# A fixed issue order for TensorE, VectorE and ScalarE in the first stage of a Mamba, attention and mixture-of-experts layer

## The chip, the cores and the metric

The kernel runs on one core of a Trainium2 chip. That core has a matrix engine (TensorE, PE in the profile), a vector engine (VectorE, DVE), a scalar engine for activations (ScalarE, ACT), a general engine (GpSimd, POOL) and a synchronising engine (SyncE, SP) whose queue issues nearly all transfers here. Each engine takes its own list of instructions[...]. The metric is the time of one execution on the device in microseconds (us); less is better. The time before is the median of three executions, 5567.89 us (5564.01 to 5571.6).

## The reference, cut to what matters

Eight sequences of 512 tokens with 512 features pass through three blocks, each followed by a residual sum and a layer norm. Everything is in 32-bit floats.

```python
x = _layernorm(x + mamba(x))             # state-space block
x = _layernorm(x + attention(x, ctx))    # 16 heads of 32, keys and values from ctx
x = _layernorm(x + moe(x))               # 32 experts, 4 per token, capacity 640, plus a shared expert
```

The state-space block projects to 1024 inner channels and a gate, convolves over four taps, forms a step size `dt` (a softplus), and runs a recurrence over the tokens for 1024 channels times 16 states, then gates and projects back:

```python
dA = exp(A[None, None] * dt[..., None]);  dBx = dt[..., None] * B_ssm[:, :, None, :] * x_main[..., None]
h = dA_t * h + dBx_t                     # token by token
y_t = einsum('bdn,bn->bd', h, C_t)
y = (y + x_main * D) * silu(z);  out = y @ out_proj_w + residual
```

The expert block takes a softmax over 32 logits, keeps four of eight groups and four experts in them, numbers the tokens of each expert in order, and drops those beyond 640.

## The kernel before, in words

`program` (from L1423) opens three stages in turn: `layers` (state-space block, attention, gate, shared expert), `experts` (the 32 experts) and `finish` (the last layer norm). Only `layers` is touched by the change.

**The main loop of `layers`.** The tokens are cut into 16 chunks of 256, two per sequence. A chunk is walked in 32 steps; a step handles 128 channels (`c = 2*q + ci`) and four states (`g`). One step is: `carry` (ACT, L443: the incoming state into column 0 of a buffer `h`, of which there are four), `decays` (ACT, L437: four exponentials for the *next* step into one of two buffers `l_da`), `scan` (DVE, L449 product, L453 the recurrence, and in the first chunk of a sequence L455, a copy of the last state), then other work, and last `collect` (DVE, L470: `h` times C in place; PE, L474: four products that sum over the states into the PSUM tile `py`, of which there is one; in the first state group also two products at L462).

**The other work of a step** is of two kinds, and stands in the text between `scan` and `collect`. Some belongs to the same chain: for the chunk before, `back` (PE, L503, steps 1 and 2) with its residual sum and layer norm (DVE L512, then L74 to L78, ACT L57, L58, L80); for this chunk, `gate_x` (PE L302, steps 3 to 6); for the chunk after, `norm_x` (step 9), `flip_x` (step 11), `convolve` (steps 12, 15, 18, 21: PE L302, then ACT L322 and L328, then six taps on DVE, L336), `silu` (step 23), `x_proj` (step 24); and every eighth step `prepare` (PE L389, then seven ACT instructions, L399 to L405, then four on DVE, L409 to L412, whose results transfers spread over `both`). The rest are the *units* of the sequence before, made by `units` (L706): queries, score maxima (PE L766, DVE L768), their negation (PE L775, ACT L779), weights (PE L792, ACT L796), weighted sums (PE L808, ACT L820), division (ACT L837, L838, DVE L839 to L841), output (PE L703, DVE L856, L857), the gate (`choose`, DVE L546 to L602; `locate`, DVE L620 to L635) and the shared expert (PE L703, DVE L883, L897). A budget of weights, one number per unit, decides how many units fall into each step, so that they end with the second chunk. The units of the last sequence follow after the main loop, with no scan beside them.

**How a unit is written down.** `do` (L1006) issues a unit's matmuls and then runs what was left over of the units before, so that the reading of a PSUM tile stands one unit behind its matmuls; `settle` runs what is left and keeps what that returns in turn; `dry` repeats until nothing is left. `settle` also stands right ahead of `collect`:

```python
            h = carry(t, 2 * q + ci, g)
            ...
            scan(t, 2 * q + ci, g, f["ready", q][1], bc, das[n % 2], h)
            ...                      # back, gate_x, prepare, convolve, units: each through do()
            settle()
            collect(2 * q + ci, g, h, bc, py, f)
```

PSUM: two buffers `mm` for projections and most units, two buffers `sc` for scores and weights, one `po`, one `py`.

**What sets the order.** The text of the kernel is not the order of the queues. The framework collects all instructions with what they depend on, and its scheduler plays the program through with its own estimates of durations; an engine takes next, among the instructions that are ready in that estimate, the one that stands first in the text. What comes out is one fixed list per engine, which the chip then follows. `silu` (L350) and its return to the table of exponentials (L354) are tied by `keep_in_program_order` behind what was written before them on ACT; nothing ties later instructions behind them. Transfers of `layers` are issued by SP (and the scattered ones by POOL), in an order that the same scheduler sets.

## Time and profile before

| | |
|---|---|
| median of three executions | 5567.89 us (5564.01 to 5571.6) |
| profiled execution, its own time | 5569.36 us |
| its span, first to last instruction | 5567.7 us |
| first scan starts, last scan ends (DVE L453) | 72.2 us, 3691.1 us |
| last product of the main loop ends (PE L474) | 3694.5 us |
| `layers` ends, `experts` begins | about 3947 us |
| PE busy over the span | 4880.6 us (88%) |
| DVE busy over the span | 4349.5 us (78%) |
| ACT busy over the span | 2592.1 us (47%) |
| granted TensorE clock, mean | 0.937 |

In the profile a line such as `L470 DVE TENSOR_TENSOR h<-h,bc` names the line of the kernel, the engine, the operation, and what is written from what. The timeline gives, for each merged group, its start, its length from first start to last end, and, in square brackets, the idle time of the engine just before it and what ended that. A matmul in 32-bit floats stands in the records as two, so that the four products of `collect` are eight.

### The profile page before, as it was taken

How to read it: one execution, taken by the hardware profiler on the slowest of the kernel's cores; microseconds unless marked ns; L12 is line 12 of the kernel's file. 1: busy time of each engine (PE TensorE's matmuls, PEld its weight loads, DVE VectorE, ACT ScalarE, POOL GpSimd, SP SyncE). 2: the span in 40 equal slices, each digit the busy share in tenths (PEclk: the TensorE clock that was granted, in tenths of full speed). 3: DMA queues.
4: the chain of work that ended last, by engine and by line, in shares of the span. 5: the costliest groups of instructions: out<-in, count | busy, mean ns of one | idle time of the engine just before them, and what ended most of it. 6: DMA issues, size and time to landing. Idle time of an engine off the chain costs nothing. (4 is left out here: it accounts for less than half of the span.)

```text
span 5567.7 us, 60361 instructions
## 1 busy us (share of the span) xinstructions
PE 4880.6 (88%) x19752; PEld 2718.5 (49%) x19752; DVE 4349.5 (78%) x5738; ACT 2592.1 (47%) x5481; POOL 569.2 (10%) x424
## 2 busy tenths in 40 slices
PE   6668889888888988888898898879899999999994
PEld 4334344334434434443443443333577777777773
DVE  6998899989889999898989999864466565555554
ACT  4555555655566455555555656523222222222223
POOL 1000002001100200200020020010111111111111
PEclk8778999999999999999999999989999999999997
DMA  6787355444634634643463454441345454544444
GB/s 187 226 229 211 109 137 176 121 118 143 178 106 112 201 97 129 184 124 108 122 207 98 120 188 113 112 158 45 96 125 126 124 126 119 126 125 120 119 121 145
DMA packets 554282, 769.83 MB, mean 138 GB/s; under 512 B 135754, under 2 KB 268394, under 8 KB 551920
## 3 DMA queue, kind: packets, MB, share of 16 engines
q1 hardware_dynamic: 517952, 677.55, 41.6%
q0 software_dynamic: 33280, 76.90, 7.4%
q10 hardware_dynamic: 2736, 11.54, 0.5%
q8 instruction: 156, 2.56, 0.2%
q14 instruction: 158, 1.29, 0.1%
HBM read 508.68 MB, written 165.05 MB: 121 GB/s over the span
## 5 line engine op out<-in xcount | busy, mean ns | idle before, releaser
L437 ACT ACTIVATE l_da<-both,l_aneg 128x256 f32<-128x256 f32 x2048 | 888.4, 499 | 790.6 <-DVE h L453 745.9
L453 DVE TENSOR_TENSOR_SCAN h<-l_da,h 128x1028 f32<-128x1028 f32 x512 | 1170.0, 2292 | 50.7 <-ACT h L443 27.3
L474 PE MATMUL py<-h,l_twice 128*64 128x256 f32 x4096 | 627.5, 421 | 195.1 <-DVE h L470 194.9
L449 DVE TENSOR_TENSOR h<-both,bc 128x1024 f32<-128x1024 f32 x512 | 617.9, 1214 | 142.5 <-PE py L474 81.6
L470 DVE TENSOR_TENSOR h<-h,bc 128x1024 f32<-128x1024 f32 x512 | 622.6, 1219 | 6.3 <-DMA l_ka<-filld 0.3
L474 PEld LDWEIGHTS py<-h,l_twice 128*64 128x64 f32 x4096 | 292.5, 147 | 568.8 <-issue 237.7
L1220 PE MATMUL ps_h<-xT,w 128*128 128x320 f32 x1536 | 435.6, 433 | 0.0
L766 PE MATMUL ps_s<-l_ka,l_qa 64*128 64x512 f32 x1024 | 314.1, 692 | 137.4 <-DVE mx L768 137.2
L1300 POOL DMA_INDIRECT based<-y,xe x160 | 252.1, 1576 | 1313.5 <-ACT y L1323 571.3
L1241 DVE TENSOR_TENSOR hT<-ps_h,p 128x320 f32<-128x320 f32 x128 | 62.9, 492 | 379.0 <-PE ps_h L1220 379.0
L768 DVE TENSOR_REDUCE mx<-ps_s 128x2 f32<-128x1024 f32 x256 | 310.4, 1216 | 55.4 <-PE ps_s L766 54.7
L1220 PEld LDWEIGHTS ps_h<-xT,w 128*128 128x128 f32 x1536 | 292.2, 190 | 118.2 <-issue 0.4
L792 PE MATMUL ps_t<-l_qa,l_ka 64*128 64x512 f32 x1024 | 299.6, 648 | 20.9 <-ACT eT L796 17.5
L796 ACT ACTIVATE eT<-ps_t 128x1024 f32<-128x1024 f32 x256 | 259.1, 1013 | 110.1 <-PE ps_t L792 109.6
L808 PE MATMUL po<-eT,l_va 128*64 128x512 f32 x1024 | 281.4, 629 | 24.5 <-ACT raw L820 20.8
L641 POOL DMA_INDIRECT xbuf<-x2t,dest x128 | 218.8, 1709 | 814.6 <-DVE dest L635 776.2
L1220 PE MATMUL ps_h<-t,s 128*128 128x320 f32 x1024 | 286.1, 432 | 0.0
L302 PE MATMUL ps_z<-xnT,wm 128*128 128x256 f32 x1024 | 240.9, 389 | 17.4 <-DVE o L512 16.4
L302 PE MATMUL ps_x<-xnT,wm 128*128 128x256 f32 x1024 | 245.6, 394 | 11.1 <-DMA wm<-in_in_proj_w 10.1
L703 PE MATMUL ps_p<-x2T,wa 128*128 128x512 f32 x512 | 243.9, 625 | 11.8 <-DVE hT L883 10.3
L503 PE MATMUL po<-wm,zs 128*128 128x512 f32 x512 | 236.9, 613 | 9.8 <-DVE k L688 5.3
L1220 PEld LDWEIGHTS ps_h<-t,s 128*128 128x128 f32 x1024 | 194.6, 190 | 81.1
(234 smaller groups left out, 7422.5 us busy)
## 6 DMA issues: line engine op xcount, KB each, us to landing
bc<-scr SPq DMA_DIRECT2D x1024, 128.0 KB
w<-in_w SPq DMA_DIRECT2D x93, 1024.0 KB
wm<-in_in_proj_w SPq DMA_DIRECT2D x128, 512.0 KB
xbuf<-zero SPq DMA_DIRECT2D x32, 1362.5 KB
xe<-xbuf SPq DMA_DIRECT2D x32, 1362.5 KB
both<-dt SPq DMA_DIRECT2D x256, 128.0 KB
both<-dtx SPq DMA_DIRECT2D x256, 128.0 KB
wm<-in_out_proj_w SPq DMA_DIRECT2D x64, 512.0 KB
```

The lines of the kernel that those rows point to most:

```text
L302: nc.tensor.matmul(ps[:, i, :], w[:, dc, i * P : (i + 1) * P], f["xnT"][:, dc, :], start=(dc == 0), stop=(dc == DC - 1),)
L437: nc.scalar.activation(da[:, n, 1:], dt[:, c % 2, j, :], AF.Exp, scale=aneg[:, c, j, g, m : m + 1])
L449: nc.vector.tensor_tensor(steps, dtx[:, c % 2].unsqueeze(2).to_broadcast([P, 2, NG // 2, T]), bc[0], ALU.mult)
L453: nc.vector.tensor_tensor_scan(flat, da.rearrange("p n t -> p (n t)"), flat, 0.0, ALU.mult, ALU.add)
L470: nc.vector.tensor_tensor(steps, steps, bc[1], ALU.mult)
L474: nc.tensor.matmul(py[j * HP : (j + 1) * HP, c % 2, :], twice, h[:, j * 2 + m, 1:], start=False, stop=(s == (NST // NG - 1, NG // 2 - 1, 1)),)
L766: nc.tensor.matmul(ps[:, j, :], qa[r, lt * P : (lt + 1) * P], ka[r, :], start=True, stop=True)
L768: return lambda: nc.vector.tensor_reduce(mx[:, lt, :].unsqueeze(2), ps, AX.X, ALU.max) and None
L792: nc.tensor.matmul(ps[:, j, :], ka[r, kc * P : (kc + 1) * P], qa[r, :], start=True, stop=True)
L796: nc.scalar.activation(eT, ps, AF.Exp)
L808: nc.tensor.matmul(po[j * 2 * HD : (j + 1) * 2 * HD, :], va[:, kc, i, j * HD : (j + 2) * HD], eT[:, j, :], start=(kc == 0), stop=(kc == SC ...
L1220: nc.tensor.matmul(ps, w[:, n, r * P : (r + 1) * P], x[:, n, :], start=not more and n == 0, stop=n == 1, skip_group_check=more,)
```

## The change

One line opens a region around `layers`. Inside it each of the three engines named issues its instructions in the order in which the text emits them. The order of SP and POOL, and what happens across engines, stays with the framework's scheduler. No instruction, buffer or transfer of the kernel's text is added or removed.

```diff
         with ExitStack() as ctx:
+            ctx.enter_context(tc.manual_schedule(engines={mybir.EngineType.Activation, mybir.EngineType.DVE, mybir.EngineType.PE}))
             layers(ctx, tc, a, x1d, filld, based, xbuf)
         with ExitStack() as ctx:
             experts(ctx, tc, a, xbuf, based)
```

## The prediction

> **What bounds the kernel now.** First the busy time by stretch: the main loop from the end of chunk 1 to the end of chunk 14, chunk 15, the units of the last sequence, then experts and the last norm.

> ```profile
> core 0: us, PE busy (x) PEld busy (x) DVE busy (x) ACT busy (x) POOL busy (x), PEclk, DMA share, GB/s
> 430.50:3490.50 3060.00, 2671.08 (x10948) 1264.56 (x10946) 2778.62 (x3222) 1746.64 (x3677) 251.58 (x179) 0.94 0.49 140
> 3490.50:3694.50 204.00, 169.46 (x711) 77.75 (x709) 181.35 (x202) 103.57 (x222) 0.00 (x0) 0.93 0.39 107
> 3694.50:3947.00 252.50, 223.44 (x714) 89.34 (x712) 102.39 (x195) 65.55 (x86) 30.98 (x35) 0.92 0.32 106
> 3947.00:5568.00 1621.00, 1536.98 (x6272) 1134.14 (x6272) 925.94 (x1724) 453.31 (x978) 253.04 (x161) 0.97 0.48 123
> ```

> In the loop DVE is busy 2778.62 of 3060 us (91%) and PE 2671.08 (87%): two engines near their limit, only 281 us of idle DVE to be had. A step takes (3694.5 - 430.5) / 448 = 7.3 us, a pair of chunks 466 us.

> Then the order in which the two run, from the timeline of a chunk's first steps, PE and then DVE:

> ```profile
> 1623.62 7.13 PE L503 MATMUL po<-wm,zs 128*128 128x512 f32 x16
> 1630.68 0.65 PE L462 MATMUL py<-xs,l_ident 128*64 128x256 f32 x4
> 1631.17 1.03 PE L474 MATMUL py<-h,l_twice 128*64 128x256 f32 x8
> 1632.13 7.13 PE L503 MATMUL po<-wm,zs 128*128 128x512 f32 x16
> 1639.19 1.08 PE L474 MATMUL py<-h,l_twice 128*64 128x256 f32 x8
> 1640.21 3.72 PE L302 MATMUL ps_z<-xnT,wm 128*128 128x256 f32 x16
> ```
> ```profile
> 1635.92 1.23 DVE L470 TENSOR_TENSOR h<-h,bc 128x1024 f32<-128x1024 f32 x1
> 1637.59 0.75 DVE L512 SCALAR_TENSOR_TENSOR o<-po,l_rs,o 128x512 f32<-128x512 f32 x1 [0.45 <-PE po L503]
> 1638.37 0.69 DVE L74 BATCH_NORM_STATS2 st<-o 128x6 f32<-128x512 f32 x1
> ...
> 1645.49 0.15 DVE L60 TENSOR_TENSOR m<-v,r 128x2 f32<-128x2 f32 x1
> ...
> 1646.27 0.16 DVE L78 SCALAR_TENSOR_TENSOR less<-mv,o 128x2 f32<-128x2 f32 x1
> ```

> PE runs without a gap, and in the order of the text. It can, because the product L470 that it needs at 1639.19 was done at 1637.15, before the norm (L512 to L78), though the text puts L470 of step 2 behind that norm. DVE mixes the norm with later scans up to 1646.4. Counting through the trace, the k-th L470 ends a median of 14.5 us (two steps) ahead of the k-th group of L474; set against the text's order, L449, L453 and L470 stand 11 to 14 places early on DVE and the readings of PSUM (L768) 9 late; PE keeps the text's order within 4 places in the mean. So the scheduler gives the scan chain a lead of two to three steps, held in the four buffers `h`, and it is this lead that keeps PE from waiting. In the same stretch L474 waited for L470 only so long:

> ```profile
>   PEld py L474: 79.7, 19
>   PE py L474: 70.6, 16
> ```

> [...] in this window ACT sat 4.75 us before `l_da` for the scan, with ready work later in its list. A list in a bad order therefore stalls. [...]

> **The change part by part.** No instruction goes or comes save table loads; three lists are re-ordered.

> *Table loads.* Now exponentials slip between the four `silu` of a chunk:

> ```profile
> L353 ACT ACT_TABLE_LOAD x60 | 77.0, 1283 | 1.0
> L354 ACT ACT_TABLE_LOAD x40 | 51.3, 1283 | 0.7
> L796 ACT ACT_TABLE_LOAD x14 | 18.0, 1283 | 0.2
> L437 ACT ACT_TABLE_LOAD x13 | 16.7, 1283 | 0.2
> ```

> With six at L549 these are 133. In the text's order each of the 40 groups needs one load out and one back, 80: 53 x 1.283 = 68 us less of ACT. ACT is busy 57% of the loop, so most of it lies beside DVE; I put it into the steps below (two loads a group) and credit it nowhere else.

> *The scan's lead.* In the text's order DVE runs, per step, L449 1.22 + L453 2.30 (+ L455 0.17), then the readings of this step's units, then L470 1.22; PE runs the products of the step before (1.05), then this step's units; ACT runs carry 0.2 and decays 2.0 and then its readings. So with D the end of the last L470: PE starts its units at D + 1.1, DVE reaches the readings at D + 3.6, and L470 must wait for the last unit that DVE reads. The next units wait in turn for L470. Where PE is late without a reading on DVE, the lateness goes over to the next step. Four kinds of step show the sum:
> - *Back and norm* (steps 1, 2): PE 2 x (1.05 + 7.13) + 0.65 = 17.0; then DVE 2 x (0.75 + 0.69 + 0.18) + 0.17, ACT and hops 0.7, DVE 0.8, L470 1.22 = 6.1, with PE idle: 23 us for two steps.
> - *Prepare*: PE ready at D + 2.0, seven ACT instructions 4 x 0.47 + 3 x 0.63 = 3.8 behind the decays, to D + 6.1; DVE 4 x 0.68 = 2.7; L470: 10.0, and 11 to 13.6 with a convolution or maxima beside it.
> - *Convolve with taps in the same step*: PE 1.1 + 3.7, ACT 1.8, taps 6 x 0.48 = 2.9, L470: 10.7.
> - *Attention*: PE 1.1 + five units of 1.1, the last a maximum, then 1.2 + 1.2: 8.4 to 9.

> Walking the 64 steps of a pair in the text's order with these rows (projection unit 3.4, `choose` 104.1 / 8 = 13.0, `locate` 4.4) gives, first chunk: 5.5, 4.8, 18.2, 13.4, 4.8, 4.8, 4.8, 4.8, 6.1, 9.4, 9.8, 12.5, 4.8, 7.7, 4.8, 4.8, 8.4, 7.6, 13.2, 13.6, 8.6, 10.7, 8.4, 6.0, 12.0, 7.4, 8.4, 11.2, 12.1, 6.9, 8.5, 9.0 = 273. Second: 7.4, 4.7, 19.0, 4.7, 8.7, 4.7, 4.7, 5.9, 11.0, 12.1, 6.8, 11.2, 10.7, 8.7, 4.7, 12.7, 14.6, 11.2, 4.7, 17.3, 4.7, 4.7, 28.7 (`choose`, with the taps and lateness before it), 4.7, 7.0, 8.8, 6.4, 10.7, 11.4, 6.4, 6.4, 6.4 = 292. Together 565, against 466.

> *ACT behind PE.* A carry stands behind the ACT readings of the step before, and the scan needs it; where PE is late by more than a microsecond the next scan is held. Going through the list: +21 a pair; so 586. [...] So a pair costs +99 to +144, taken +120.

> *The rest.* Seven pairs: 7 x 120 = +840. The first pair has no attention and takes 358 us from the first scan; its backs, prepares and taps cost +20 to +80, taken +50. The last sequence's units: PE busy 223 of 252 us in nearly the text's order, -10 to +50, taken +20. Experts and last norm, 1621 us: unchanged.

> *Queues left to the scheduler.* SP's 3056 transfers of this stage are the same. Now DVE waits 14.9 us for `bc` and 40.0 for `both` in the whole run (idle before L449); longer steps give them more time, and a load placed behind one whose buffer comes free late could cost as much again: 55, taken 0. POOL's two small copies per convolution (L319/L321, 1.58 us, ahead of ACT L328) lie beside PE's 3.7; should they be late, ACT's whole list waits, and with it the carry and the scan: up to 1.6 x 64 = 100 us, taken 0. Not seen in this trace is how the granted clock answers: in its first tenth PE is 69% busy at clock 0.82; the new loop would have PE at about 70%. At 0.82 PE's legs grow by 0.94 / 0.82 - 1 = 15%; they set about a third of a pair's 586: 0.15 x 190 = 28 a pair, 200 in all; at the other end nothing. Taken 0, kept for the upper end.

> Sum, against the profiled execution's own 5569.36 (its span is 5567.7, its time 1.5 above the median, which is noise): 5569 + 840 + 50 + 20 = 6479, say **6480**. The loop's ends: 7 x 99 + 20 - 10 = +703, 6272; 7 x 144 + 80 + 50 = +1138, 6707; with clock, POOL and SP 7060.

> **Rivals.**
> 1. *Lockstep*, the above: 6200 to 6800. Chance 0.73.
> 2. *Half of it is absorbed.* Four buffers `h`, and steps whose units DVE doesn't read, still let DVE run ahead; only norms, prepares and `choose` cost: per pair 2 x 6 + 8 x 3 + 15 = 51, so 5569 + 7 x 51 + 50 = 5976; 5600 to 6200. For it: the walk lets no wait overlap that I put in series. Against: 23 of the 32 steps of a pair's second chunk have a reading on DVE. Chance 0.15.
> 3. *Clock and ACT's list make it worse*: beyond 6800, about 6950. The first tenth's 0.82 speaks for it. Chance 0.07.
> 4. *Faster.* The scheduler's estimates are not the chip's durations: its list has 2.0 us stalls of the scan behind the carry where tables are exchanged, and PE waits 129 us for maxima (L766 for L768), which the text's order reads sooner. If 68 us of loads and those 129 us went, and the lead were not needed: about 5370. It decides only where the lead costs less than 200 us, 13 us per chunk; the norm alone has 6 and the prepares 12. Chance 0.04.
> 5. *No change*, since the lists were nearly those of the text: DVE's has only 2170 of 3994 instructions in a common order. Chance 0.01.

> **How the numbers follow.** A measurement of this kernel tells 0.2% (11 us) from no change. Faster 0.04, same 0.01, slower 0.95. The range 6050 to 6820 holds nearly all of 1 and a part of 2, and leaves out faster, the milder two thirds of 2 and the worst of 3: about 0.2.

> **What would show it.** Right: experts still 1621 us; a pair near 586; DVE's share in the loop from 91% to 72%, PE's to about 70%; L474 and its weight loads waiting for L470 many hundreds of us instead of 150; DVE waiting for PE's units, for `xs` of ACT (L336) and for `dt` (L409); 80 table loads. Wrong: a lead of L470 over L474 that stays above 5 us; SP or POOL named as the main releaser; a tail far from 250.

## The result

6674.41 us (the median of four runs, 6663.69 to 6680.88) against 5565.95 us of the kernel before: a ratio of 1.1999 (95% interval 1.1984 to 1.2013), slower by 1108 us. The forecast was 6480, with 6050 to 6820 as its range.

Busy time of the kernel after by stretch, the same four stretches as shown of before (chunks 2 to 14, chunk 15, the units of the last sequence with a few us of the next stage, the rest):

```profile
core 0: us, PE busy (x) PEld busy (x) DVE busy (x) ACT busy (x) POOL busy (x), PEclk, DMA share, GB/s
513.50:4522.00 4008.50, 2969.96 (x10954) 1353.85 (x10954) 2866.57 (x3214) 1672.46 (x3610) 156.29 (x179) 0.86 0.36 105
4522.00:4815.30 293.30, 207.33 (x745) 91.39 (x746) 207.23 (x234) 108.98 (x236) 19.39 (x15) 0.85 0.33 91
4815.30:5060.00 244.70, 205.14 (x676) 81.05 (x676) 95.98 (x171) 65.51 (x86) 18.13 (x21) 0.91 0.29 96
5060.00:6675.30 1615.30, 1536.85 (x6272) 1134.56 (x6272) 925.45 (x1724) 452.66 (x978) 251.90 (x160) 0.97 0.48 123
```

The loop took it all. Chunks 2 to 15 went from 3264.0 us (430.5 to 3694.5) to 4301.8 (513.5 to 4815.3), +1038, 148 per pair; the first pair from 430.5 to 513.5, +83. From the loop's end to the first load of the experts' tokens it is 238 us instead of 253, and the experts and the last norm are as before. In chunks 2 to 14 DVE fell from 91% to 72% busy, PE from 87% to 74%, and the granted clock from 0.94 to 0.86. PE's busy time in chunks 2 to 15 rose all the same, from 2840.5 to 3177.3 us for the same matmuls (the trace before lacks 40 of some 11700 records). So of the 1038 us, about 337 are longer busy time of PE and 701 longer idle time.

The start of chunk 8 in the timeline, PE first and then DVE, the same steps as the prediction shows of before (steps 1 and 2, and the start of 3):

```profile
2370.16 8.54 PE L503 MATMUL po<-wm,zs 128*128 128x512 f32 x16
2378.63 0.65 PE L462 MATMUL py<-xs,l_ident 128*64 128x256 f32 x4
2379.11 1.03 PE L474 MATMUL py<-h,l_twice 128*64 128x256 f32 x8
2380.07 7.13 PE L503 MATMUL po<-wm,zs 128*128 128x512 f32 x16
2392.46 1.97 PE L474 MATMUL py<-h,l_twice 128*64 128x256 f32 x8 [5.26 <-DVE h L470]
2394.37 4.96 PE L302 MATMUL ps_z<-xnT,wm 128*128 128x256 f32 x16
```
```profile
2376.77 0.17 DVE L455 COPY l_state<-h 128x4 f32<-128x4 f32 x1
2385.53 0.75 DVE L512 SCALAR_TENSOR_TENSOR o<-po,l_rs,o 128x512 f32<-128x512 f32 x1 [8.59 <-PE po L503]
2387.24 0.75 DVE L512 SCALAR_TENSOR_TENSOR o<-po,l_rs,o 128x512 f32<-128x512 f32 x1 [0.97 <-PE po L503]
...
2391.10 0.16 DVE L78 SCALAR_TENSOR_TENSOR less<-mv,o 128x2 f32<-128x2 f32 x1
2391.18 1.23 DVE L470 TENSOR_TENSOR h<-h,bc 128x1024 f32<-128x1024 f32 x1
```

DVE waits 8.59 us for PE's product, and then PE waits 5.26 us for DVE's norm and for L470 behind it. The two work by turns, where before both ran through. And PE comes out of its wait slow: L474 takes 1.97 us instead of 1.08, L302 4.96 instead of 3.72 (from 2392.4 to 2400 us the granted clock was 0.70, from 2379 to 2387.2, ahead of the wait, 1.00).

Waits of PE and DVE that grew most, and the one of ACT that grew most, over the whole run: engine and line, what it waited for, us in total, times, longest. Waits of POOL and five more of ACT's that grew by 150 us and more are left out.

```profile
PEld py L474 <- DVE h L470: 1292.9, 406, 13.9
PE py L474 <- DVE h L470: 1010.6, 343, 13.1
ACT eT L796 <- PE ps_t L792: 544.6, 194, 7.9
DVE h L453 <- ACT h L443: 388.4, 136, 10.3
DVE mx L768 <- PE ps_s L766: 189.5, 119, 3.4
DVE dtx L409 <- ACT dtx L405: 166.8, 51, 9.7
DVE o L512 <- PE po L503: 140.9, 32, 11.6
```

PE's matmuls alone stood 1011 us before L474 (195 before the change). The median distance from the end of L470 to the start of its L474, called the lead below, fell from 14.5 us to 0.06.

### The profile page after: what moved, and what is told of

The parts are those of the page before. It is cut to its first block, busy times and chain, and to the rows that moved or that the text cites. A ratio compares the mean times of both kernels' runs of the same rounds, so it can differ in the third digit from the quotient of the medians.

```text
span 6675.3 us, 60400 instructions
## 1 busy us (share of the span) xinstructions
PE 5211.7 (78%) x19752; PEld 2823.0 (42%) x19752; DVE 4477.4 (67%) x5738; ACT 2519.6 (38%) x5428; POOL 460.9 (7%) x424
## 5 line engine op out<-in xcount | busy, mean ns | idle before, releaser
L474 PE MATMUL py<-h,l_twice 128*64 128x256 f32 x4096 | 700.0, 472 | 1011.4 <-DVE h L470 1010.6
L453 DVE TENSOR_TENSOR_SCAN h<-l_da,h 128x1028 f32<-128x1028 f32 x512 | 1177.4, 2300 | 427.3 <-ACT h L443 388.4
L437 ACT ACTIVATE l_da<-both,l_aneg 128x256 f32<-128x256 f32 x2048 | 872.2, 498 | 498.7 <-DVE h L453 496.5
L474 PEld LDWEIGHTS py<-h,l_twice 128*64 128x64 f32 x4096 | 294.7, 161 | 1460.3 <-DVE h L470 1292.9
L449 DVE TENSOR_TENSOR h<-both,bc 128x1024 f32<-128x1024 f32 x512 | 623.3, 1217 | 7.5 <-DMA bc<-scr 7.5
L470 DVE TENSOR_TENSOR h<-h,bc 128x1024 f32<-128x1024 f32 x512 | 624.0, 1219 | 5.4
L796 ACT ACTIVATE eT<-ps_t 128x1024 f32<-128x1024 f32 x256 | 260.9, 1019 | 544.7 <-PE ps_t L792 544.6
L768 DVE TENSOR_REDUCE mx<-ps_s 128x2 f32<-128x1024 f32 x256 | 309.4, 1219 | 189.8 <-PE ps_s L766 189.5
L766 PE MATMUL ps_s<-l_ka,l_qa 64*128 64x512 f32 x1024 | 310.0, 692 | 59.0 <-DVE mx L768 47.2
L792 PE MATMUL ps_t<-l_qa,l_ka 64*128 64x512 f32 x1024 | 320.0, 701 | 36.5 <-DMA l_qa<-nm 20.9
L808 PE MATMUL po<-eT,l_va 128*64 128x512 f32 x1024 | 303.5, 674 | 19.6 <-ACT raw L820 19.4
L703 PE MATMUL ps_p<-x2T,wa 128*128 128x512 f32 x512 | 304.4, 755 | 5.5 <-ACT x2T L870 4.8
L302 PE MATMUL ps_x<-xnT,wm 128*128 128x256 f32 x1024 | 268.1, 421 | 11.5 <-DMA wm<-in_in_proj_w 11.2
L302 PE MATMUL ps_z<-xnT,wm 128*128 128x256 f32 x1024 | 273.3, 426 | 0.0
L336 DVE SCALAR_TENSOR_TENSOR xs<-xp,l_cw,xs 128x256 f32<-128x256 f32 x384 | 180.0, 482 | 110.0 <-ACT xs L328 100.9
L302 PEld LDWEIGHTS ps_z<-xnT,wm 128*128 128x128 f32 x1024 | 215.0, 216 | 68.8 <-issue 27.3
L302 PEld LDWEIGHTS ps_x<-xnT,wm 128*128 128x128 f32 x1024 | 211.3, 212 | 72.2 <-issue 36.5
```

Of the source, the lines that this page charges most:

```text
L302: nc.tensor.matmul(ps[:, i, :], w[:, dc, i * P : (i + 1) * P], f["xnT"][:, dc, :], start=(dc == 0), stop=(dc == DC - 1),)
L437: nc.scalar.activation(da[:, n, 1:], dt[:, c % 2, j, :], AF.Exp, scale=aneg[:, c, j, g, m : m + 1])
L449: nc.vector.tensor_tensor(steps, dtx[:, c % 2].unsqueeze(2).to_broadcast([P, 2, NG // 2, T]), bc[0], ALU.mult)
L453: nc.vector.tensor_tensor_scan(flat, da.rearrange("p n t -> p (n t)"), flat, 0.0, ALU.mult, ALU.add)
L470: nc.vector.tensor_tensor(steps, steps, bc[1], ALU.mult)
L474: nc.tensor.matmul(py[j * HP : (j + 1) * HP, c % 2, :], twice, h[:, j * 2 + m, 1:], start=False, stop=(s == (NST // NG - 1, NG // 2 - 1, 1)),)
```

## The experiments

Every run below but the last two is one profiled execution, timed beside the kernel before on the same chip (5561 to 5565 us). The last two were timed four and five times, and the times of one of them lie 28 us apart; so a difference of 30 us or less between single executions tells nothing. Where the text of the kernel is changed, all it computes stays.

### One engine at a time

```diff
-engines={mybir.EngineType.Activation, mybir.EngineType.DVE, mybir.EngineType.PE}
+engines={mybir.EngineType.DVE}          # only_act, only_pe likewise
```

> Only VectorE issues in the text's order; ScalarE and TensorE are left to the scheduler. Lead theory (the loss comes from L470 standing behind the readings of its step's units on VectorE): most of the loss comes back, 6350 to 6650 us, L474 and its weight loads waiting for L470 over 1000 us. ScalarE theory (the carry behind ScalarE's readings makes the loss): below 5900 us. TensorE theory (its own order makes the loss): below 5700 us.

> Only ScalarE issues in the text's order. Lead theory: the carry and the decays stand behind the ScalarE readings of the step before, so the scan may run ahead by less than a step and part of the lead is lost, but L470 need not wait for units: 5700 to 6000 us, table loads 80. ScalarE theory: most of the loss, above 6300 us. If the saved table loads decide: below 5550 us.

> Only TensorE issues in the text's order, which it nearly had. Lead theory: 5520 to 5640 us, the lead of L470 over L474 stays above 8 us. TensorE theory: above 6000 us.

| held to the text | time us | over before | PE and its weight loads idle until L470, us | lead of L470, median us |
|---|---|---|---|---|
| none (before) | 5566 | | 429 | 14.5 |
| DVE | 5801 | +239 | 759 | 0.05 |
| ACT | 5709 | +147 | 804 | 0.06 |
| PE | 5735 | +173 | 261 | 18.7 |
| all three | 6674 | +1108 | 2304 | 0.06 |

The last column but one adds the waits of two rows of one engine, matmuls and weight loads, which overlap in time. It shows where PE waits, and is not time lost.

No engine's order by itself makes the loss; the sum of the three is 559, half of it. (With DVE held the time lies in the band of the ScalarE theory, but ACT held gives 5709 where that theory needed 6300. That time lies at the foot of the lead theory's band. PE held misses its band by 95 us without coming near the 6000 of the TensorE theory.) The lead theory as stated falls with two rows: DVE held to the text, and ACT held too, take the whole lead away, and cost a fifth and an eighth of the loss. PE's list shows how that can be. In the run with DVE alone the scheduler lists L474 on average 8.7 matmul records (four to five matmuls) later than in the run with all three held, and puts the next projections ahead of it, even within one projection:

```profile
1728.59 3.62 PE L302 MATMUL ps_z<-xnT,wm 128*128 128x256 f32 x16
1732.14 1.13 PE L389 MATMUL ps_dt<-xd,l_w_dt 32*128 32x256 f32 x4
1733.19 1.13 PE L302 MATMUL ps_z<-xnT,wm 128*128 128x256 f32 x4
1734.26 1.08 PE L474 MATMUL py<-h,l_twice 128*64 128x256 f32 x8
1735.27 2.86 PE L302 MATMUL ps_z<-xnT,wm 128*128 128x256 f32 x12
1738.74 1.08 PE L474 MATMUL py<-h,l_twice 128*64 128x256 f32 x8 [0.62 <-DVE h L470]
```

This is the norm of a chunk's start again: PE does 5.7 us of other matmuls (1728.59 to 1734.26) and then L474 of step 2, with no idle time ahead of it. PE held alone cost more than its near agreement with the text let me expect. There DVE runs further ahead and stops more often for lack of `h` buffers (L449 waits 209.5 us for L474, 81.6 before); that this is all of its 173 us is not shown:

```profile
DVE h L449 <- PE py L474: 209.5, 65, 13.7
```

ACT in the text's order has 83 table loads of 1283 ns in the whole run (counted in the kernel after; 80 of them in this stage, as expected) instead of 136, and held alone it is slower all the same.

### Two engines at a time

> VectorE and TensorE in the text's order, ScalarE left to the scheduler. Single engines cost 239 (VectorE) and 173 us (TensorE). Two-sided theory (VectorE's list puts L470 behind the readings, and TensorE's list puts the next step's units behind the products of L474; either engine alone can still be given the slack, both together wait for each other by turns): far more than 239 + 173 = 412, 6250 to 6550 us. Sum theory (each engine's order costs for itself): 5974, 5930 to 6020 us.

> ScalarE and TensorE in the text's order, VectorE left to the scheduler. Two-sided theory: the carry behind ScalarE's readings of the step before keeps the scan within a step, and TensorE cannot go round it, but L470 need not wait for the readings on VectorE: more than the sum, 5950 to 6250 us. Sum theory: 147 + 173, 5882, 5840 to 5930 us.

> ScalarE and VectorE in the text's order, TensorE left to the scheduler. Two-sided theory: TensorE can be listed with the next units ahead of L474, so the sum or less: 5850 to 6000 us. Sum theory: 147 + 239, 5948, 5900 to 6000 us. If TensorE's order hardly mattered: as all three, 6674.

| held to the text | time us | over before | sum of the single ones | PE and its weight loads idle until L470, us |
|---|---|---|---|---|
| DVE, PE | 6484 | +923 | 412 | 2117 |
| ACT, PE | 6042 | +480 | 320 | 980 |
| ACT, DVE | 5830 | +269 | 386 | 708 |

The excess over the sum stands where PE is one of the two: +511 with DVE, +160 with ACT, and -117 without PE (20 us under the band that I had given it). For DVE and PE the tile `l_twice`, which L474 reads, shows nearly the wait of the full change (2303.6):

```profile
  DVE h L470: 2117.2, 679
```

So most of the loss, 923 of 1108, is made by two lists that hold each other: DVE's puts L470 behind the readings of units that PE has yet to do, PE's puts the next units behind L474. With PE freed the scheduler finds the slack there (+269). With DVE freed it finds part of it: ACT and PE held still cost 480, and where the 160 above their sum arise was not followed.

### Giving the slack back in the text

With all three engines held, one half of `collect` moved. First DVE's half, L470, straight behind the scan (line numbers shift: L470 becomes L459, L474 L476):

```diff
             scan(t, 2 * q + ci, g, f["ready", q][1], bc, das[n % 2], h)
+            weight_h(h, bc)             # L470, taken out of collect
             ...                         # units, settle()
             collect(2 * q + ci, g, h, bc, py, f)
```

> All three in the text's order, but the text is changed in one place: the VectorE half of collect (L470) stands straight behind the scan, ahead of the step's other work; the TensorE half stays behind it. Lead theory: TensorE no longer waits for L470 behind readings, the lead is one step's other work; 5750 to 6150 us, the waits of L474 for L470 below 300 us, what is left being the carry behind ScalarE's readings and the late VectorE chains. Clock theory (the lower granted clock makes most of the loss): little changes unless TensorE's share rises, above 6300 us. ScalarE theory: above 6300 us.

6112.7 us: 562 of 1108 us come back with one DVE instruction moved ahead of the step's other work. The wait of PE's matmuls for it fell from 1011 to 331 us, not quite below the 300 expected (with the weight loads 801):

```profile
PE py L476 <- DVE h L459: 330.9, 156, 12.2
```

Then PE's half one step later. DVE's order stays but for the gating product (L486), which needs `py` and moves behind L470 in one step of eight:

```diff
             settle()
             weight_h(h, bc)             # L470 where it was
-            collect(2 * q + ci, g, h, bc, py, f)
+            if late: late.pop()()       # L474 of step k-1; then gating, new py
+            late.append(lambda a=(2 * q + ci, g, h, bc, py, f): collect(*a))
```

> All three in the text's order; VectorE's and ScalarE's order of the changed kernel is kept (L470 behind the readings of its step), and only the TensorE half of collect (L474, with L462 and the gating that need py) stands one step later, behind the next step's units. Two-sided theory: giving TensorE the slack instead of VectorE brings back about as much as the runs that moved VectorE's work did (6113 and 6060): 5950 to 6200 us, L474 and its weight loads waiting for L470 below 400 us. If it is VectorE's order by itself: no gain, above 6500 us.

5961.1 us, 713 us back, from moving TensorE's side and the gating. The matmuls wait 176.7 us for L470, with the weight loads 408, just over the 400 expected:

```profile
PE py L476 <- DVE h L459: 176.7, 56, 12.3
```

L470 stands behind the readings of its step here as in the full change. So that place on DVE does not make most of the loss by itself; the pair does.

Then the scan chain (carry, decays, scan, L470) one whole step ahead of the units, and a version of it with three waits taken away:

```diff
-            h = carry(...); decays(...); scan(...)          # of step k
+            ahead(s + 1)                # carry, decays, scan, L470 of step k+1
             ...                         # units of step k
             collect(2 * q + ci, g, hs.pop(s), None, py, f)
```

> All three in the text's order, with the text changed: carry, decays, scan and L470 of step k+1 stand ahead of step k's other work, and L474 of step k behind it, so that L470 has a lead of one whole step. Two-sided theory: one of the two sides has its slack back, 5620 to 5900 us, L474 waiting for L470 below 200 us, the scan waiting for the carry below 150 us. If the late chains inside the units (norm, prepare, taps) make most of the loss: above 6000 us.

> As lead1 (all three in the text's order, scan chain one step ahead), with its three largest new waits taken away: the gating (L486) stands ahead of the scan of the next step, the carry one further step ahead, and L470 of step k+1 behind the readings of step k. If those waits (TensorE at L462 for the gating 148 us, the scan for the carry 206, TensorE for the maxima 149 + 50) are what is left of the loss: 5700 to 5900 us. If what is left is that any order in fixed blocks leaves waits elsewhere: 5950 to 6100 us.

`lead1` gave 6060.5 us. That is above its band and in that of the rival, that late chains inside the units make most of the loss. A whole step's lead therefore doesn't suffice, and gives back hardly more (52 us) than moving L470 alone did. The lead is there (median 8.8 us), and between 500 and 4200 us PE's matmuls stood 9.5 us in all for L459; but other waits took the place, in the same stretch:

```profile
DVE h L453 <- ACT h L443: 206.1, 109, 8.1
PE ps_s L768 <- DVE mx L770: 148.8, 50, 5.2
PE py L466 <- DVE zs L488: 148.4, 27, 14.2
```

PE now waits for readings that stand behind 4.9 us of scan work on DVE (L768 for the maxima, of which PSUM holds two; L466 for the gating that frees `py`). `lead1b` removes the first and most of the third and gives 5906.3 us, a hair above one band and below the other, so it decides between neither: 154 us came back, 341 stay. What these 341 us are is not settled. Up to the last L476 PE is busy 97 us longer than before (3217.0 against 3120.2) and idle 255 us longer. The waits are spread (141.6 us L476 for L459, 133.5 for the maxima, 98.6 for the norm after attention, 76.6 for its division), and no run took them away one by one.

### ScalarE's order with a lead

```diff
+engines={mybir.EngineType.Activation}    # the texts of lead1 and lead1b
```

> The text of lead1, but only ScalarE held to it; VectorE and TensorE left to the scheduler. If ScalarE's order alone cost 147 us because the carry stands behind the readings of the step before, the carry now has a step's lead, the exponentials' table is loaded 83 times instead of 136, and it ends at or below the kernel before: 5450 to 5600 us. If ScalarE's readings of units behind the decays were the cost: 5650 to 5750 us.

> The text of lead1b (carry two steps, scan chain one step ahead of the units), only ScalarE held to it. If what ScalarE's order still costs in lead1_act (96 us) is the carry behind the readings of the step before (the scan waited 194 us for it there), that wait falls below 80 us and the time to 5480 to 5590 us, 80 table loads, equal to the kernel before or a little faster. If ScalarE's order costs through other waits (readings behind decays that wait for the scan, L474 waiting for L470): 5620 to 5700 us.

Ratios 1.0166 (1.0142 to 1.0191) and 1.0177 (1.0163 to 1.0191), 96 us each, both in the bands of the theory that ACT's order costs through other things than the carry's place. The carry's wait (193.9 us in the first) was taken away in the second, and it moved to the decays beside it:

```profile
DVE h L453 <- ACT l_da L437: 184.8, 86, 8.5
```

I read this so that ACT's list costs through what it queues ahead of the scan chain, whichever of its members that hits, and that the 53 table loads saved (68 us of ACT) don't pay for it. But these texts were not run with no engine held, so how much of the 96 us is ACT's list and how much the new text is not shown. No version beat the kernel before.

## Why the prediction was right, and where not

**The sum of the loop.** Right in kind, low in size. Walked: 565 a pair, 586 with ACT behind PE. The range's top of +144, 610 a pair, has up to 24 more for the hops between engines, an estimate of the author that the trace before does not show: there DVE and ACT, where they had waited for another engine, started a median of 33 to 48 ns after the end of what they waited for (the loop, waits over 100 ns), PE's matmuls 53 to 54 ns. Measured: 4301.8 / 7 = 614.5. Steps 1 and 2, put at 23 us, took 24.1 in the mean of the first chunks; the first chunk of a pair was put at 273 and took 301, the second 292 and 313 (means over chunks 2 to 15). Single steps, from the end of one group of L474 to that of the next, came out between 4.7 us under and 6.6 us over their rows, so part of the nearness is errors that cancel.

**The terms that were mis-sized.** "At 0.82 ... 28 a pair ... Taken 0": the clock did fall, to 0.86, and the term was worth more. PE's 337 us of longer busy time are 48 a pair. The clock records account for most of them: in chunks 2 to 15 PE was busy for 960 us at half clock, and for 320 before. In the kernel after, matmul records of L302 start a median of 216 ns apart at full clock and 427 at half, those of L703 429 and 854; so half of the difference, 320 us, is an estimate from these of what the slow matmuls cost. How much of it lies on the path isn't separated. If all 48 us lay there, the walk with ACT would come to 634 a pair, 20 too many. So the nearness of the range's top, 610, to 614.5 is partly luck. "ACT behind PE, +21": in chunks 2 to 15 the scan waited 349 us for the carry, 50 a pair (27 us, 4 a pair, before), though this overlaps other waits, and the 21 can't be read off it. The first pair, +83, was 3 us over its upper end; the tail, -14, under its lower end of -10.

**"No instruction goes or comes save table loads ... credit it nowhere else".** Right: 80 loads of 1283 ns in the stage, all tied to `silu`, and the run with ACT alone shows that the saving is not worth its order.

**"It is this lead that keeps PE from waiting".** This step failed as a statement of cause. With DVE alone held the lead was gone (0.05 us) and the loss 239 us. The walk had the other half in it ("The next units wait in turn for L470"), but the prediction didn't say that the loss hangs on it; the number came out because the change holds both lists. The rival "half of it is absorbed" falls with the result. So does "faster": even ACT's order by itself, which saves the table loads, costs 147 us.

**Two readings of the trace before.** The L470 at 1635.92 is not the one that the L474 at 1639.19 needs. Counted through the trace that L474 is of step 2 and its L470 ended at 1612.75; the one shown is of step 5. The lead was thus 26 us there, and the argument gains by it. And in the 4.75 us that ACT sat before `l_da`, what stood next in its list was not ready: the carry at 1632.29 came right behind the L474 that frees its buffer, from 1631.17 to 1632.2. An order that holds ready work back shows at 1655.45: L425 had waited for DVE, and L348 behind it ran at 1656.27, though its product had ended at 1654.32.

**The signs named beforehand.** DVE 72% (measured 71.5), PE about 70% (74), L474 with its weight loads waiting many hundreds of us (2304), DVE waiting at L409 and L336 (167 and 101 us): as said. The loop hardly waited for transfers: L449 7.5 us, L792 20.9, and at most 32.3 at one line (ACT L837).

## What to carry to other kernels

Before pinning the order of several engines (fixing it to the text), find for each pair of instructions across two queues which of the two lists holds the slack. In this kernel pinning one engine left the scheduler the other, pinning both took the slack away, and the costs didn't add (239 + 173 became 923). Where a text says "produce, other work, consume" and becomes the queue itself, move one half of the consumer across a block of other work: here one moved instruction gave back half the loss. And count for TensorE, beside each wait, the slow matmuls that follow it: here L474's took a mean of 687 ns after gaps of 4 us and more, and 430 after gaps of 0.5 to 1.5 us.

## What the runs showed of the hardware

The clock's answer to gaps was sharper than the mean of 0.86 tells. Of the records of L474 in the kernel after that followed an idle gap of PE of 4 us or more, all 84 took over 500 ns (mean 687); after gaps of 0.5 to 1.5 us none of 42 did (all 430); between 1.5 and 4 us 45 of 188 did. Gaps of 3.5 us and more before L474 went from 21 to 109.
